# Layer 1 experts of a two-layer metaformer: token tiles loaded in quarters of channels and turned by VectorE in squares of 32

## The chip, the cores and the metric

The kernel runs on one core of a Trainium2 chip. The metric is the device time of one execution in microseconds (us); lower is better. A core has five engines, each working through its own queue of instructions in order: TensorE (PE in the profile) multiplies matrices, VectorE (DVE) and ScalarE (ACT) work elementwise, GpSimd (POOL) does odd work and issues indirect DMAs, and SyncE (SP) issues ordinary DMAs. They wait for each other through semaphores. SBUF is the on-chip memory of 128 partitions, PSUM the banks that TensorE writes.

## The reference, cut to what matters

```python
# layer 1, after a selective scan; x is [4, 256, 32, 32], t its tokens [4 * 1024, 256]
t = t + _L1_ffn_ref(_ln_t(t), Wr, br, ln_g, ln_b, W1, b1, W2, b2)

def _L1_ffn_ref(x, ...):            # 8 experts, 256 channels, 1024 hidden
    logits = xt @ Wr + br
    top_p, top_idx = jax.lax.top_k(softmax(logits), 2)
    weights = top_p / top_p.sum(axis=-1, keepdims=True)
    xn = (xt - mu) * rsqrt(var + 1e-5)
    xe = xn[None] * ln_g[:, None] + ln_b[:, None]
    h = gelu(xe @ W1[e] + b1[e])
    y = h @ W2[e] + b2[e]
    out = weighted sum of y of the two experts of each token
```

The kernel works an expert only on the tokens that chose it.

## The kernel before

Layer 0 and the scan of layer 1 take the first 3362 us and are left alone but for one copy (below). Tokens live channels-first; `norm()` subtracts the mean, turns 128 tokens at a time with TensorE into PSUM (`nm_tp`, L1701), copies them to `tok` with ScalarE (L1705), squares them for the variance (`nm_sq`, L1709) and makes the two factors `nm_s` with powers on GpSimd (`nm_ve`, `nm_s`, L1713 to L1721); ScalarE then scales `tok` (L1725). `route()` picks the two best experts with some fifty small VectorE instructions and an exp on ScalarE (L1605 to L1678), and works out a slot for each token and choice. `scatter()` (L1981) writes rows of 258 numbers (256 channels, and two that say where the result goes) to their slots in DRAM, `slots_x`, with 16 indirect DMAs for each of the 4 batches. Batches 0 to 2 are normalised, routed and scattered during the scan.

A tile is a block of T = 256 slots of one expert. 17 early tiles need only the first three batches. Between them the last batch is normalised, routed and scattered, as a generator (`routing`) that is stepped six times after each early tile. Then come 19 late tiles, and three that run only if a count asks for them.

For each tile, `slots()` loads 256 slots of 258 numbers with one DMA of 258 KB (`xa` for early, `xs` for late tiles; all 17 early loads are issued up front, each with its own buffer). `weights()` loads the expert's w1 and w2 of 1 MB each and its small vectors, two tiles ahead. `inputs()` turns the slots into channels-first with four TensorE transposes (`tp`, L2254) into PSUM, and VectorE applies the expert's gain and shift in two instructions, one for each 128 channels (`xe`, L2257), and works out the result's row numbers `to` (L2260). `hidden()` is 32 matmuls `hp` (L2269) and 8 Gelus `hid` (L2271); `result()` is 32 matmuls `yp` (L2277), one VectorE addition `ys` (L2280), and two indirect DMAs by GpSimd to `results` (L2282), of which the second waits for the first. At the end `results` is loaded again, weighted, turned and added to x.

The order within each queue is set when the program is built: a scheduler places the instructions, starting from the order in which the code calls them.

Of the kernel before, what the change touches and what calls it, by code (L numbers as in the profile page):

```python
# [21 lines left out]
P = 128  # L22
# [15 lines left out]
NS = 16  # L38
SCALE = KD ** -0.5
T = 256  # L40
NTILE = 2 * B * L // T + E - 1
USUAL = 2 * B * L // T + E // 2
BLOCKS = B * L // T
# [19 lines left out]
def metaformer(ctx: ExitStack, tc: tile.TileContext, t: dict, out: bass.AP):  # L63
# [168 lines left out]
    class Routing0:  # L232

        def __init__(self, b, bank, space):
            self.b, self.bank, self.space = b, bank, space
# [236 lines left out]
    with ExitStack() as st:  # L472
# [393 lines left out]
        class Pair:  # L866
# [41 lines left out]
            def norm(self):  # L908
                if self.g == 0 and self.a == 0:
                    self.image.att = wk.tile([P, CT, L], F32, tag="att", name="att")  # L910
                rden = p2.tile([P, L], F32, tag="w", name="rden", bufs=1)[:, : 2 * P]
                nc.vector.reciprocal(rden, self.o_ps[:, 1])
                nc.vector.tensor_tensor(self.image.att[:, self.g, ts(self.a, 2 * P)], self.o_ps[:, 0], rden, ALU.mult)
# [682 lines left out]
    def route(b, tok, slot, space, psum, tag):  # L1596
# [74 lines left out]
        else:  # L1671
# [5 lines left out]
            ends = late.fill(room, tiles, done)  # L1677
            nc.vector.tensor_scalar(extra, ends[0:1, E - 1 : E], USUAL - EARLY + 0.5, None, ALU.is_gt)  # L1678

    def norm(b, tok, pool, psum, tag, raw_tag, d):  # L1680

        rw = rw1
        for h in range(NHALF):
            cols = ts(h, HALF)
            mean = psum.tile([P, HALF], F32, tag=tag, name="nm_mean")
            for c in range(CT):
                nc.tensor.matmul(mean, mean_w, x[b][:, c, cols], start=(c == 0), stop=(c == CT - 1))  # L1689
            yield  # L1690
            for c in range(CT):
                nc.vector.tensor_tensor(d[:, c, cols], x[b][:, c, cols], mean, ALU.subtract)
            yield
        var = pool.tile([P, NT], F32, tag="nm_var", name="nm_var")
        for r in range(NT // 2):
            tp = psum.tile([P, 2, C], F32, tag=tag, name="nm_tp")
            raw = psum.tile([P, HALF], F32, tag=raw_tag, name="raw")[:, : 2 * E].rearrange("p (n e) -> p n e", e=E)
            for i in range(2):
                n = 2 * r + i
                for c in range(CT):  # L1700
                    nc.tensor.transpose(tp[:, i, ts(c, P)], d[:, c, ts(n, P)], ident)  # L1701
                for c in range(CT):
                    nc.tensor.matmul(raw[:, i], d[:, c, ts(n, P)], rw[:, c, :], start=(c == 0), stop=(c == CT - 1))  # L1703
            yield
            nc.scalar.copy(tok[:, ts(r, 2), :C], tp)  # L1705
            for i in range(2):
                n = 2 * r + i
                squares = pool.tile([P, C], F32, tag="nm_sq", name="nm_sq")
                nc.scalar.activation(squares, tp[:, i], AF.Square, scale=C ** -0.5, accum_out=var[:, n : n + 1])  # L1709
            nc.scalar.copy(lg1[:, ts(r, 2)], raw)  # L1710
            yield
        ve, s1, s2 = (pool.tile([P, NT], F32, tag=f"nm_{i}", name=f"nm_{i}") for i in ("ve", "s1", "s2"))
        nc.gpsimd.tensor_scalar(ve, var, 1e-5, None, ALU.add)  # L1713
        nc.gpsimd.tensor_tensor(s1, ve, minus_half, ALU.pow)  # L1714
        yield
        yield
        nc.gpsimd.tensor_tensor(ve, s1, s1, ALU.mult)
        nc.gpsimd.tensor_tensor(ve, ve, var, ALU.mult)
        nc.gpsimd.tensor_scalar(ve, ve, 1e-5, None, ALU.add)
        nc.gpsimd.tensor_tensor(s2, ve, minus_half, ALU.pow)  # L1720
        nc.gpsimd.tensor_tensor(s2, s2, s1, ALU.mult)  # L1721
        nc.vector.tensor_tensor(lg1, lg1, s1.unsqueeze(2).to_broadcast([P, NT, E]), ALU.mult)
        yield
        for n in range(NT):
            nc.scalar.mul(tok[:, n, :C], tok[:, n, :C], s2[:, n : n + 1])  # L1725
        yield
# [247 lines left out]
    nc.vector.memset(count, 0.0)  # L1974
    nc.vector.memset(done, 0.0)

    def scatter(b):

        for n in range(NT):
            for k in range(2):  # L1980
                nc.gpsimd.indirect_dma_start(  # L1981
                    out=slots_x, out_offset=bass.IndirectOffsetOnAxis(ap=slot[:, k, n : n + 1], axis=0),
                    in_=tok[:, n], in_offset=None)
                yield


    with ExitStack() as st:
# [22 lines left out]
        class Scan:  # L2010
# [29 lines left out]
            def inputs(self):  # L2040

                if not self.k:
                    self.uu = lead.uu
                    return
                self.uu = p2.tile([P, 2, L], F32, tag="uu", name="uu")
                nc.gpsimd.tensor_tensor(self.uu[:, 0], self.prep.dx[:, self.c], self.bb, ALU.mult)  # L2046
                nc.scalar.copy(grid(self.uu[:, 1]), cols_flipped(self.uu[:, 0]))
# [166 lines left out]
    with ExitStack() as st:  # L2214
        of_tiles = st.enter_context(ExitStack())
        pb = of_tiles.enter_context(tc.tile_pool(name="m1_b", bufs=2))
        blocks = slots_x.rearrange("(k a p) c -> k p a c", a=T // P, p=P)

        class Tile:
            def __init__(self, tiles, i, tag="xs", bufs=4):  # L2220
                self.tiles, self.i = tiles, i
                self.xs = pb.tile([P, T // P, W], F32, tag=tag, name=tag, bufs=bufs)

            def register(self, k, most):
                return nc.values_load(self.tiles.which[0:1, k, self.i : self.i + 1], engines=[mybir.EngineType.SP],
# [2 lines left out]

            def slots(self):
                block = self.register(1, E * BLOCKS)  # L2230
                nc.sync.dma_start(self.xs, blocks[bass.ds(block, 1)].rearrange("o p a c -> p (o a) c"))

            def weights(self):
                e = self.register(0, E - 1)
# [10 lines left out]
                self.b2 = pb.tile([P, C], F32, tag="b2e", name="b2e")  # L2245
                nc.sync.dma_start(self.b2, t["b2_1"][bass.ds(e, 1)].rearrange("o d -> (o d)").partition_broadcast(P))

            def inputs(self, ps_t):


                tp = ps_t.tile([P, CT, T], F32, tag="tp", name="tp")
                for a in range(T // P):
                    for c in range(CT):
                        nc.tensor.transpose(tp[:, c, ts(a, P)], self.xs[:, a, ts(c, P)], ident)  # L2254
                self.xe = pb.tile([P, CT, T], F32, tag="xe", name="xe")
                for c in range(CT):
                    nc.vector.tensor_scalar(self.xe[:, c], tp[:, c], self.lng[:, c : c + 1],  # L2257
                                            self.lnb[:, c : c + 1], ALU.mult, ALU.add)
                self.to = pb.tile([P, T // P], I32, tag="to", name="to", bufs=NTILE)
                nc.vector.scalar_tensor_tensor(self.to, self.xs[:, :, C + 1], self.tiles.expert[:, self.i : self.i + 1],  # L2260
                                               self.xs[:, :, C], ALU.not_equal, ALU.add)

            def hidden(self, ps_h):
                self.hid = pb.tile([P, NF, T], F32, tag="hid", name="hid")
# [21 lines left out]
        with ExitStack() as sa:  # L2286
            pa = sa.enter_context(tc.tile_pool(name="m1_a", bufs=1))
            psa = sa.enter_context(tc.tile_pool(name="m1_psa", bufs=1, space=PSUM))
            ps_t = sa.enter_context(tc.tile_pool(name="m1_ps_t", bufs=2, space=PSUM))
            ps_h = sa.enter_context(tc.tile_pool(name="m1_ps_h", bufs=3, space=PSUM))  # L2290
            ps_y = sa.enter_context(tc.tile_pool(name="m1_ps_y", bufs=1, space=PSUM))

            def run(one_tile):
                one_tile.inputs(ps_t)
                one_tile.hidden(ps_h)
                one_tile.result(ps_y)

            todo = [Tile(early, i, "xa", EARLY) for i in range(EARLY)]
            for i in range(EARLY):
                todo[i].slots()  # L2300
                if i < 2:
                    todo[i].weights()
            b = B - 1
            routing = chain(norm(b, tok, pa, psa, "t", "raw", pa.tile([P, CT, L], F32, tag="nm_d", name="nm_d")),
                            route(b, tok, slot, pa.tile([P, NUMBERS], F32, tag="numbers", name="numbers"), psa, "t"), scatter(b))
            for i in range(EARLY):
                run(todo[i])
                if i + 2 < EARLY:
                    todo[i + 2].weights()
                for _ in range(6):  # L2310
                    next(routing, None)
            assert next(routing, "end") == "end"

            def run_late(which):
                for i in which:
                    one_tile = Tile(late, i)
                    one_tile.slots()
                    one_tile.weights()
                    run(one_tile)

            run_late(range(USUAL - EARLY))
            more_tiles = nc.values_load(extra[0:1, 0:1], min_val=0, max_val=1,
                                        skip_runtime_bounds_check_because="a comparison gives 0 or 1")
            with tc.If(more_tiles > 0):
                run_late(range(USUAL - EARLY, NTILE - EARLY))
# [97 lines left out]
```

## Time and profile before

| | us |
|---|---|
| median of 3 runs | 3963.53 (3959.7 to 3966.43) |
| the profiled execution, own time | 3952.81 |
| its span | 3951.0 |
| expert stage, first load to last yp | 3362 to 3903 |
| PE busy, of 481 us (3422 to 3903) | 475.0 |
| DVE, ACT, POOL busy, of the same | 58.1, 123.0, 78.8 |
| TensorE transposes tp, x144 | 0.273 each |
| granted TensorE clock, whole span | 0.876 |
| granted TensorE clock, 3422 to 3903 | 1.00 |

A row of the page's list of groups has the line, the engine, the operation, output and input names with shape, and the count; then the group's busy time in us and the mean of one in ns; then the idle time of the engine just ahead of such instructions and what ended most of it. A line of the timeline has the start in us, the length in us, the same names, and in brackets the idle time before it with its releaser. A timeline line with "x32" is 32 instructions in a row; its length reaches to the end of the last one, which overlaps the start of what follows, so spacing is read from starts.

### The profile page before, as it was taken

How to read it: one execution, taken by the hardware profiler on the slowest of the kernel's cores; microseconds unless marked ns; L12 is line 12 of the kernel's file. 1: busy time of each engine (PE TensorE's matmuls, PEld its weight loads, DVE VectorE, ACT ScalarE, POOL GpSimd, SP SyncE). 2: the span in 40 equal slices, each digit the busy share in tenths (PEclk: the TensorE clock that was granted, in tenths of full speed). 3: DMA queues.
4: the chain of work that ended last, by engine and by line, in shares of the span. 5: the costliest groups of instructions: out<-in, count | busy, mean ns of one | idle time of the engine just before them, and what ended most of it. 6: DMA issues, size and time to landing. Idle time of an engine off the chain costs nothing. (4 is left out here: it accounts for less than half of the span.)

```text
span 3951.0 us, 49637 instructions
## 1 busy us (share of the span) xinstructions
PE 3373.9 (85%) x17330; PEld 1889.9 (48%) x17330; DVE 3017.3 (76%) x5164; ACT 2789.5 (71%) x3738; POOL 1936.6 (49%) x1675
## 2 busy tenths in 40 slices
PE   8378888888788888886697889998998989999996
PEld 5134444534353444543475333443443433788885
DVE  3689899989989898999476899999999999211112
ACT  2889999899989999996244677777767766322222
POOL 0145544675648475575343766556555556121111
PEclk9567887788778777788798999999999999999997
DMA  9400084000000000000384434334334334755555
GB/s 283 121 1 1 1 230 128 1 1 31 12 1 1 1 33 1 1 12 17 97 243 133 142 119 139 118 107 127 120 112 127 125 112 128 223 183 185 189 192 188
DMA packets 241814, 393.71 MB, mean 100 GB/s; under 512 B 31888, under 2 KB 182160, under 8 KB 241424
## 3 DMA queue, kind: packets, MB, share of 16 engines
q1 hardware_dynamic: 218016, 340.54, 28.4%
q0 software_dynamic: 19904, 48.48, 3.8%
q8 instruction: 139, 2.28, 0.2%
q10 hardware_dynamic: 3632, 1.40, 0.1%
q14 instruction: 123, 1.01, 0.1%
HBM read 280.41 MB, written 109.94 MB: 99 GB/s over the span
## 5 line engine op out<-in xcount | busy, mean ns | idle before, releaser
L825 POOL TENSOR_SCALAR dr<-s_n,last 128x1024 bf16<-128x1024 f32 x250 | 715.6, 2880 | 729.5 <-DVE state L853 421.5
L735 ACT ACTIVATE junk_a<-s_n,state 128x1024 int8<-128x1024 f32 x448 | 514.7, 1149 | 23.6 <-DVE state L859 7.3
L2081 POOL TENSOR_TENSOR da_c<-prod,come 128x1024 f32<-128x1024 f32 x128 | 257.5, 2012 | 378.8 <-DVE h L2087 322.7
L739 DVE TENSOR_SCALAR_CACHE_REDUCE junk_v<-s_n,state 128x1024 int8<-128x1024 f32 x320 | 408.6, 1277 | 8.8
L2271 ACT ACTIVATE hid<-hp,b 128x256 f32<-128x256 f32 x288 | 134.1, 474 | 361.1 <-PE hp L2269 361.1
L786 DVE SCALAR_TENSOR_TENSOR w<-s_n,win 128x1024 f32<-128x1024 f32 x256 | 352.0, 1375 | 5.3
L789 DVE MAX8 win<-w 128x8 f32<-128x1024 f32 x256 | 314.5, 1228 | 8.8
L2070 DVE TENSOR_TENSOR_SCAN sum<-da,uu 128x1024 f32<-128x1024 f32 x127 | 289.7, 2281 | 26.5 <-PE sum L2052 19.1
L2092 PE MATMUL sum<-h,ident 128*128 128x512 f32 x512 | 261.4, 635 | 55.6 <-DVE h L2087 52.4
L893 ACT ACTIVATE ex<-sT 128x1024 f32<-128x1024 f32 x256 | 246.9, 1016 | 82.9 <-PE sT L885 82.6
L2046 POOL TENSOR_TENSOR uu<-dx,bb 128x1024 f32<-128x1024 f32 x127 | 303.6, 2390 | 1.7 <-DMA bb<-bc_d 1.6
L735 ACT ACTIVATE junk_a<-s_n,guess 128x1024 int8<-128x1024 f32 x256 | 294.2, 1149 | 7.2
L2063 DVE TENSOR_TENSOR_SCAN h<-da,uu 128x1024 f32<-128x1024 f32 x127 | 288.1, 2269 | 1.0 <-POOL uu L2046 1.0
L2087 DVE TENSOR_TENSOR_SCAN h<-da_c,uu 128x1024 f32<-128x1024 f32 x127 | 288.5, 2272 | 0.0
L2058 PE MATMUL sum<-da_c,ident 128*128 128x512 f32 x512 | 257.2, 626 | 27.3 <-POOL da_c L2081 23.8
L903 PE MATMUL o_ps<-ex,vT 128*32 128x256 f32 x2048 | 236.2, 450 | 50.1 <-ACT ex L893 35.7
L2280 DVE TENSOR_TENSOR ys<-yp,b2e 128x512 f32<-128x512 f32 x36 | 24.9, 691 | 325.7 <-PE yp L2277 325.7
L2030 ACT ACTIVATE da_c<-delta,a_log 128x1024 f32<-128x1024 f32 x128 | 268.0, 2094 | 5.2 <-DMA rows_y<-ys 5.1
L2269 PE MATMUL hp<-xe,w 128*128 128x256 f32 x1152 | 259.0, 383 | 9.4 <-DVE xe L2257 5.9
L2282 POOL DMA_INDIRECT results<-ys,to x72 | 69.3, 963 | 397.0 <-DVE ys L2280 183.6
L769 ACT COPY s_n<-sp 128x1024 f32<-128x1024 f32 x256 | 245.5, 1003 | 23.7 <-PE sp L761 16.0
L2277 PE MATMUL yp<-w2e,hid 128*128 128x256 f32 x1152 | 255.6, 380 | 0.0
(675 smaller groups left out, 7513.9 us busy)
## 6 DMA issues: line engine op xcount, KB each, us to landing
cb<-bc_d SPq DMA_DIRECT2D x128, 512.0 KB, 4.1
bb<-bc_d SPq DMA_DIRECT2D x127, 512.0 KB, 5.0
w<-in_w SPq DMA_DIRECT2D x36, 1024.0 KB, 5.4
w2e<-in_w SPq DMA_DIRECT2D x36, 1024.0 KB, 5.5
slots_x<-zeros SPq DMA_DIRECT2D x1, 33669.0 KB
slots_x<-zeros SPq DMA_DIRECT2D x1, 33282.0 KB
w<-in_w SPq DMA_DIRECT2D x72, 256.0 KB, 3.2
xs<-slots_x SPq DMA_DIRECT2D x36, 261.0 KB, 3.4
```

Source lines behind the costliest of these rows:

```text
L735: nc.scalar.activation(junk, self.row(r), AF.Sign, bias=thr, scale=-1.0, accum_out=u)
L739: nc.vector.tensor_scalar(junk, self.row(r), thr, None, ALU.is_lt, ALU.add, accum_out=u)
L786: nc.vector.scalar_tensor_tensor(w, self.row(r), self.win[:, r, 0:1], self.row(r), ALU.is_gt if r < LAST_DVE else ALU.is_ge, ALU.subtract, ...
L789: nc.vector.max(out=self.win[:, r, 1:], in_=w)
L825: ins = eng.tensor_scalar(dr, self.row(r), self.last[:, r : r + 1], None, ALU.is_lt)
L2030: nc.scalar.activation(grid(self.da_c), cols_flipped(self.prep.delta[:, self.c]), AF.Exp, scale=self.decay)
L2046: nc.gpsimd.tensor_tensor(self.uu[:, 0], self.prep.dx[:, self.c], self.bb, ALU.mult)
L2063: nc.vector.tensor_tensor_scan(rows.rearrange("p r w -> p (r w)"), self.da, self.uu[:, 0], 0.0, ALU.mult, ALU.add)
L2070: nc.vector.tensor_tensor_scan(self.sum[:, ::-1], self.da[:, ::-1], self.uu[:, 0][:, ::-1], 0.0, ALU.mult, ALU.add)
L2087: nc.vector.tensor_tensor_scan(self.hs, self.da_c, self.uu[:, 1], 0.0, ALU.mult, ALU.add)
L2092: nc.tensor.matmul(cols_flipped(self.sum[:, ts(h, HALF)]), ident, grid(self.hs)[:, :, ts(h, half)], start=False, stop=False)
L2269: nc.tensor.matmul(hp[:, f % 2], self.w1[:, c, ts(f, P)], self.xe[:, c], start=(c == 0), stop=(c == CT - 1))
```

## The change

`tok` is stored with its channels reordered, in quarters: first 32 channels of the first half of 128, then 32 of the second half, and so on. ScalarE's copy becomes two copies, one for each half. A tile is loaded with four DMAs, one for each quarter, each into 32 partitions: partition = slot within a group of 32, and 8 such groups of 64 numbers along the row (runs of 256 bytes); a fifth small DMA loads the two extra numbers (`meta`). VectorE turns all of it with one transpose instruction of squares of 32 (`xt`), after which partitions are channels, and then applies gain and shift from SBUF (`xe`). The four TensorE transposes and their two PSUM banks go; `yp` gets a second buffer. There are six `xs` buffers in place of 17 and 4; five tiles' loads are issued up front and the load of tile i + 5 after tile i. The scatters are declared independent of each other. The scatters of the last batch come out of the `routing` generator and begin after the last early load is issued (i = 12). A late tile issues its weights first and its slots second.

```diff
@@ norm()
+    def quarters(a):
+        return a.rearrange("p n (q c i) -> p n c q i", c=CT, i=S)
-            nc.scalar.copy(tok[:, ts(r, 2), :C], tp)
+            for c in range(CT):
+                nc.scalar.copy(quarters(tok[:, ts(r, 2), :C])[:, :, c],
+                               tp[:, :, ts(c, P)].rearrange("p n (q i) -> p n q i", i=S))
@@ scatter()
+    def rows_of_their_own(ins, group):
+        tc.declare_no_dep(ins, group=group, reason="rows of their own")
+        tc.add_to_no_dep_group(group, ins)
-                nc.gpsimd.indirect_dma_start(
+                rows_of_their_own(nc.gpsimd.indirect_dma_start(
...
-                    in_=tok[:, n], in_offset=None)
+                    in_=tok[:, n], in_offset=None).ins, "scatter1")
@@ Tile
-        blocks = slots_x.rearrange("(k a p) c -> k p a c", a=T // P, p=P)
+        width = CT * S
+        pieces = [slots_x[:, ts(q, width)].rearrange("(k i t) c -> k t i c", i=T // S, t=S) for q in range(P // S)]
+        marked = slots_x[:, C:].rearrange("(k a p) c -> k p a c", a=T // P, p=P)
-                self.xs = pb.tile([P, T // P, W], F32, tag=tag, name=tag, bufs=bufs)
-                nc.sync.dma_start(self.xs, blocks[bass.ds(block, 1)].rearrange("o p a c -> p (o a) c"))
+                self.xs = pb.tile([P, T // S, width], F32, tag="xs", name="xs", bufs=AHEAD + 1)
+                for q in range(P // S):
+                    nc.sync.dma_start(self.xs[ts(q, S)], pieces[q][bass.ds(block, 1)].rearrange("o t i c -> t (o i) c"))
+                self.meta = pb.tile([P, T // P, W - C], F32, tag="meta", name="meta", bufs=AHEAD + 1)
+                nc.sync.dma_start(self.meta, marked[bass.ds(block, 1)].rearrange("o p a c -> p (o a) c"))
@@ inputs()
-                tp = ps_t.tile([P, CT, T], F32, tag="tp", name="tp")
-                for a in range(T // P):
-                    for c in range(CT):
-                        nc.tensor.transpose(tp[:, c, ts(a, P)], self.xs[:, a, ts(c, P)], ident)
+                xt = pb.tile([P, T // S, CT, S], F32, tag="xt", name="xt")
+                nc.vector.transpose(xt.rearrange("p i c t -> p (i c t)"), self.xs.rearrange("p i c -> p (i c)"))
                 self.xe = pb.tile([P, CT, T], F32, tag="xe", name="xe")
                 for c in range(CT):
-                    nc.vector.tensor_scalar(self.xe[:, c], tp[:, c], self.lng[:, c : c + 1],
-                                            self.lnb[:, c : c + 1], ALU.mult, ALU.add)
+                    nc.vector.tensor_scalar(self.xe[:, c].rearrange("p (i t) -> p i t", t=S), xt[:, :, c],
+                                            self.lng[:, c : c + 1], self.lnb[:, c : c + 1], ALU.mult, ALU.add)
@@ the early and late tiles
-            ps_t = sa.enter_context(tc.tile_pool(name="m1_ps_t", bufs=2, space=PSUM))
-            ps_y = sa.enter_context(tc.tile_pool(name="m1_ps_y", bufs=1, space=PSUM))
+            ps_y = sa.enter_context(tc.tile_pool(name="m1_ps_y", bufs=2, space=PSUM))
-            for i in range(EARLY):
+            for i in range(AHEAD):
                 todo[i].slots()
                 if i < 2:
                     todo[i].weights()
...
+            sending = scatter(b)
             for i in range(EARLY):
                 run(todo[i])
+                if i + AHEAD < EARLY:
+                    todo[i + AHEAD].slots()
+                else:
+                    assert next(routing, "end") == "end"
+                    for _ in range(6):
+                        next(sending, None)
                 if i + 2 < EARLY:
                     todo[i + 2].weights()
                 for _ in range(6):
                     next(routing, None)
...
             def run_late(which):
                 for i in which:
                     one_tile = Tile(late, i)
+                    one_tile.weights()
                     one_tile.slots()
-                    one_tile.weights()
                     run(one_tile)
```

More of the change, by code (lines that the diff above doesn't have):

```diff
@@ L40 @@
 T = 256
+S = 32
+AHEAD = 5
 NTILE = 2 * B * L // T + E - 1
@@ L2216, in metaformer, with __init__ @@
         pb = of_tiles.enter_context(tc.tile_pool(name="m1_b", bufs=2))
-        blocks = slots_x.rearrange("(k a p) c -> k p a c", a=T // P, p=P)
+        width = CT * S
+        pieces = [slots_x[:, ts(q, width)].rearrange("(k i t) c -> k t i c", i=T // S, t=S) for q in range(P // S)]
+        marked = slots_x[:, C:].rearrange("(k a p) c -> k p a c", a=T // P, p=P)
         class Tile:
-            def __init__(self, tiles, i, tag="xs", bufs=4):
+            def __init__(self, tiles, i):
                 self.tiles, self.i = tiles, i
-                self.xs = pb.tile([P, T // P, W], F32, tag=tag, name=tag, bufs=bufs)
             def register(self, k, most):
@@ L2246, in weights, with inputs @@
                 nc.sync.dma_start(self.b2, t["b2_1"][bass.ds(e, 1)].rearrange("o d -> (o d)").partition_broadcast(P))
-            def inputs(self, ps_t):
-                tp = ps_t.tile([P, CT, T], F32, tag="tp", name="tp")
-                for a in range(T // P):
-                    for c in range(CT):
-                        nc.tensor.transpose(tp[:, c, ts(a, P)], self.xs[:, a, ts(c, P)], ident)
+            def inputs(self):
+                xt = pb.tile([P, T // S, CT, S], F32, tag="xt", name="xt")
+                nc.vector.transpose(xt.rearrange("p i c t -> p (i c t)"), self.xs.rearrange("p i c -> p (i c)"))
                 self.xe = pb.tile([P, CT, T], F32, tag="xe", name="xe")
                 for c in range(CT):
-                    nc.vector.tensor_scalar(self.xe[:, c], tp[:, c], self.lng[:, c : c + 1],
-                                            self.lnb[:, c : c + 1], ALU.mult, ALU.add)
+                    nc.vector.tensor_scalar(self.xe[:, c].rearrange("p (i t) -> p i t", t=S), xt[:, :, c],
+                                            self.lng[:, c : c + 1], self.lnb[:, c : c + 1], ALU.mult, ALU.add)
                 self.to = pb.tile([P, T // P], I32, tag="to", name="to", bufs=NTILE)
-                nc.vector.scalar_tensor_tensor(self.to, self.xs[:, :, C + 1], self.tiles.expert[:, self.i : self.i + 1],
-                                               self.xs[:, :, C], ALU.not_equal, ALU.add)
+                nc.vector.scalar_tensor_tensor(self.to, self.meta[:, :, 1], self.tiles.expert[:, self.i : self.i + 1],
+                                               self.meta[:, :, 0], ALU.not_equal, ALU.add)
             def hidden(self, ps_h):
@@ L2288, in metaformer @@
             psa = sa.enter_context(tc.tile_pool(name="m1_psa", bufs=1, space=PSUM))
-            ps_t = sa.enter_context(tc.tile_pool(name="m1_ps_t", bufs=2, space=PSUM))
             ps_h = sa.enter_context(tc.tile_pool(name="m1_ps_h", bufs=3, space=PSUM))
-            ps_y = sa.enter_context(tc.tile_pool(name="m1_ps_y", bufs=1, space=PSUM))
+            ps_y = sa.enter_context(tc.tile_pool(name="m1_ps_y", bufs=2, space=PSUM))
             def run(one_tile):
-                one_tile.inputs(ps_t)
+                one_tile.inputs()
                 one_tile.hidden(ps_h)
                 one_tile.result(ps_y)
-            todo = [Tile(early, i, "xa", EARLY) for i in range(EARLY)]
-            for i in range(EARLY):
+            todo = [Tile(early, i) for i in range(EARLY)]
+            for i in range(AHEAD):
                 todo[i].slots()
@@ L2304, in metaformer @@
             routing = chain(norm(b, tok, pa, psa, "t", "raw", pa.tile([P, CT, L], F32, tag="nm_d", name="nm_d")),
-                            route(b, tok, slot, pa.tile([P, NUMBERS], F32, tag="numbers", name="numbers"), psa, "t"), scatter(b))
+                            route(b, tok, slot, pa.tile([P, NUMBERS], F32, tag="numbers", name="numbers"), psa, "t"))
+            sending = scatter(b)
             for i in range(EARLY):
                 run(todo[i])
+                if i + AHEAD < EARLY:
[4 more added lines that the diff above has]
+                        next(sending, None)
                 if i + 2 < EARLY:
@@ L2311, in metaformer @@
                     next(routing, None)
-            assert next(routing, "end") == "end"
+            assert next(sending, "end") == "end"
             def run_late(which):
```

## The prediction, made before the changed kernel ran

> **What bounds the kernel now.** I read the page first: its slices, its chain and its costliest groups. In the last slices TensorE (PE) is at 9 tenths while VectorE (DVE) and ScalarE (ACT) are at 1 to 3. The groups say the same:
>
> ```profile
> L2269 PE MATMUL hp<-xe,w 128*128 128x256 f32 x1152 | 259.0, 383 | 9.4 <-DVE xe L2257 5.9
> ...
> L2277 PE MATMUL yp<-w2e,hid 128*128 128x256 f32 x1152 | 255.6, 380 | 0.0
> ```
>
> 1152 is 36 tiles of 32, so 36 tiles run. Before hp PE is idle for 9.4 us in all, before yp never. The expert stage (3362 to 3903 us) is TensorE's, at a granted clock of 1.00 from 3422 us on. What TensorE does there that is no expert matmul, the timeline of a pair of tiles shows (start, length, engine, line):
>
> ```profile
> 3575.02 7.07 PE L2277 MATMUL yp<-w2e,hid 128*128 128x256 f32 x32
> 3581.92 1.04 PE L2254 MATMUL tp<-ident,xa 128*128 128x128 f32 x8
> 3583.32 7.19 PE L2269 MATMUL hp<-xe,w 128*128 128x256 f32 x32 [0.36 <-DVE xe L2257]
> 3590.35 7.07 PE L2277 MATMUL yp<-w2e,hid 128*128 128x256 f32 x32
> 3597.26 7.09 PE L2269 MATMUL hp<-xe,w 128*128 128x256 f32 x32
> ```
>
> 32 matmuls pass in 6.91 us (3590.35 to 3597.26), so a tile needs 13.83. Between 3581.92 and 3583.32 there are eight transposes, which serve two tiles at once, and 0.36 us of waiting for xe. The second tile of the pair follows with no gap. VectorE at that boundary:
>
> ```profile
> 3582.12 0.69 DVE L2280 TENSOR_TENSOR ys<-yp,b2e 128x512 f32<-128x512 f32 x1 [13.14 <-PE yp L2277]
> 3582.73 1.89 DVE L2257 TENSOR_SCALAR xe<-tp,lng,lnb 128x256 f32<-128x256 f32 x4
> ```
>
> ys starts 0.20 us after TensorE's end, xe stands behind it and starts 0.61 us later. From hp of tile 3 (3422.28) to the end of yp of tile 35 (3902.9) lie 480.6 us: 33 tiles of 13.83 are 456.4, the rest, **24.2 us**, is what transposes and xe waits cost (16 boundaries of 1.5). The one other loss is tile 2, where the last batch is routed:
>
> ```profile
> 3409.95 1.51 PE L2269 MATMUL hp<-xe,w 128*128 128x256 f32 x4 [3.46 <-ACT hid L2271]
> ...
> 3422.28 7.07 PE L2269 MATMUL hp<-xe,w 128*128 128x256 f32 x32
> ```
>
> ```profile
> 3402.74 0.96 POOL L2282 DMA_INDIRECT results<-ys,to  x1 [9.71 <-DVE ys L2280]
> 3404.01 0.24 POOL L1713 TENSOR_SCALAR nm_ve<-nm_var 128x8 f32<-128x8 f32 x1 [0.30 <-ACT nm_sq L1709]
> ...
> 3408.77 0.22 POOL L1721 TENSOR_TENSOR nm_s<-nm_s,nm_s 128x8 f32<-128x8 f32 x1
> 3409.16 1.09 POOL L2282 DMA_INDIRECT results<-ys,to  x1 [0.17 <-DVE numbers L1608]
> ```
>
> hp of tile 2 starts at 3402.01, of tile 3 at 3422.28: 20.3 us for a tile of 13.8, with a little other work, a loss of 6.9. GpSimd (POOL) does the norm's powers between the two result writes of tile 1.
>
> **What the Trainium skill says.** "VectorE: DVE Perf Modes", section The three transpose paths: VectorE turns only blocks of 32x32; 311 ns for 128x128 in bf16. No run here shows VectorE's yet. "Vector Engine (DVE) Microarchitecture Reference", section 3.8, says that the transpose sustains an element per cycle and lane. "TensorE: Matmul & The Clock Gate", Part 4, gives about 275 ns for a TensorE transpose inside a kernel; this trace has 273. Its section Why this matters for your kernels warns of TensorE idle for over some 3 us; the trace agrees: after 3.46 us of idling four hp took 1.51 us, where four otherwise take 0.86.
>
> **The change, part by part.** What decides is the order in which the built program of the changed kernel stands in each engine's queue. I read it from that program.
>
> 1. *Transposes gone from TensorE.* At most the 24.2 us above: **-24.2**.
>
> 2. *What stands ahead of xe on VectorE.* xe must now be ready when yp of the tile before ends. But ys of that tile waits for that same end, and in many tiles stands ahead of xe. Of the 33 boundaries into tiles 3 to 35:
>  - 7 have xe ahead of ys (3, 4, 14 to 18): no wait.
>  - 15 have ys, then both halves of xe (5 to 11, 13, 19, 20, 22, 23, 25, 26, 28). hp waits 0.20 to ys, 0.61 for ys, 0.41 for the first half (128x256 from SBUF to SBUF takes 0.406, the xn row at L1453), 0.06 to be seen, and 0.1 for the second: 1.4 each, 21.0.
>  - 4 have one half ahead (12, 21, 24, 27): 1.05 each, 4.2.
>  - 7 have even the new xt behind ys (29 to 35): 1.4 plus xt, to and the write of xt, on which xe waits. For xt I take 0.7: the nearest row, ys, moves 128x512 in 0.69. From below 0.6 (512 elements at that page's rate, an estimate); from above 1.3 (four times the 311 ns, an estimate). to issues in 0.15, 0.1 for the write: 2.35 each, 16.5 (15 to 21).
>
>  Together **+41.7** (33 to 48). Ahead of ys or not, an xt that isn't behind ys is hidden under 13.8 us of matmuls.
>
> 3. *Tile 2 and the routing.* Two moves. On GpSimd the second result write of tile 1 now stands ahead of nm_ve; it waits for the landing of the first (a to b is 4.7 to 5.3 us in this trace). ys of tile 1 issues about 3402.8; first write 0.95 later, its landing 5.3, second write 1.1, some 0.4 for nm_ve's waits: nm_ve at 3410.5, not 3404.01. On VectorE the whole routing chain now stands ahead of xe of tile 2, which before stood in its middle. The powers take 4.98 to nm_s; eight tok scalings on ScalarE at 0.42 come next, then a table load of 1.28 and exp, 9.9 after nm_ve; the last 29 small VectorE instructions take 4.5 as before (0.7 up to L1638 and 3.8 from L1651 on), to and half of xe 0.6. So hp of tile 2 starts at about 3410.5 + 15.1 = 3425.6, and hp of tile 3 at 3439.4, where it was 3422.28: +17.1. Of this the start (step 4) is 1.0, so **+16.1**. The cold clock after 22 us of idling: **+1** (0.65 in the row above, 0 to 2). Below: +9 if the write lands at once; above: +20.
>
> 4. *Start.* Five loads stand where one did: lnb, on which the first xe waited (1.2 us), is issued about 2.2 us later. ScalarE's table load in tile 0 hides part: **+1.0** at the end of tile 1 (0 to 3).
>
> 5. *tok in two copies.* In the scan ScalarE's tok copy (0.48 to the next) lies on a chain on which VectorE waits; a half copy adds about 0.05, in 12 places: **+0.65** (0 to 2.5).
>
> 6. *Costed at nothing.* Scatters declared independent: in the scan they wait for their place on GpSimd, not for each other. Scatters of the last batch after tile 9: the write they replace is not waited for before tile 17. Late loads with 256 B rows instead of 1032 B: issued when yp two tiles back ends, after w2, b2; w2 lands 5.6 after, I estimate the quarters at 8 to 9.5, and xe two microseconds later, where 13.8 is allowed. "DMA: Bandwidth & Descriptors", Specifications, names 512 B as the least size for line rate; no run here shows its price. Weights ahead of slots on SyncE's (SP's) queue: included. The cover is the tile of matmuls; if it is gone, see the second rival. yp in two buffers frees the bank earlier, but no yp waits now (0.0).
>
> Sum: -24.2 + 41.7 + 16.1 + 1 + 1.0 + 0.65 = **+36.2**. The profiled execution took 3952.81 (its span 3951.0), so 3989.0 in its terms; the median of the runs is 10.7 above it, so **3999.7** there, which I give.
>
> **Rivals.** *The transposes pay in full.* xe is worked out while TensorE multiplies and the routing costs what it did: -24.2 + 1.0 + 0.65 = -22.6, so 3941. For it: VectorE is busy for 58 of 481 us, so it has time. Against: it works in order, and ys can't start before yp ends. It decides if boundaries and the extra loss at tile 2 together come under 13 us, where I count 59. *Late loads come late.* If the quarters land 2 us past need at each of 19 late tiles, 38 more: 4038. For it: 1280 pieces for a tile in place of 256, with the DMA engines half busy (0.56 in this stretch). Against: 3 us of room. *It does half of what I read.* Half of the boundary waits and a routing loss of 5: 3963.5 - 24.2 + 21 + 5 + 2.6 = 3968, no change.
>
> **How the numbers follow.** The order case 0.78, with own range 3982 to 4018 (steps 2 and 3 at their ends, not both at once). Late loads 0.07. No change 0.05. Faster 0.10. The range 3966 to 4026 leaves out about 2 in 10. A measurement of this kernel tells about 0.2%, 7.9 us, from no change. Faster 0.10, within 0.2% 0.05, slower 0.85.
>
> **What would show it.** Right: no tp; hp's idle near 60 us, ended by xe; a gap of some 22 us ahead of hp of tile 2; nm_ve behind two result writes; gaps of 1.4 at tiles 5 to 13 and over 2 at tiles 29 to 35, with ys just ahead of xe or xt. Wrong: hp idle below 15 us; nm_ve within 2 us of ys of tile 1; xt waiting for xs in the late tiles; or xt over 1.3 us.

## The result, and the profile after

The changed kernel is slower: 3994.16 us at the median of 4 runs, where the kernel before has 3964.45 beside it; the ratio is 1.0075 (95% interval 1.0053 to 1.0097). 36 us were forecast and 30 came. The profiled execution took 3985.1 (span 3983.4), 32.3 more than that of before.

The costliest groups of the page after, in the lines that answer to those of before. The expert matmuls are as many and nearly as long (the mean of hp goes from 383 to 387 ns, by a slower clock in two tiles); what has grown is the idle time ahead of hp, from 9.4 to 37.5 us, and xe ends nearly all of it:

```profile
L2282 PE MATMUL hp<-xe,w 128*128 128x256 f32 x1152 | 264.1, 387 | 37.5 <-DVE xe L2270 37.4
...
L2290 PE MATMUL yp<-w2e,hid 128*128 128x256 f32 x1152 | 255.3, 379 | 0.0
```

The stage starts with the first nm_mean (3361.63 before, 3361.73 after) and ends with the last yp (3902.7 and 3934.8, each the start of its last piece and the usual spacing of 0.22), so nearly all of the difference is made in it. Below, "excess" of a tile is the time from its first hp to the next tile's first hp, less the 13.83 us of its matmuls, read off the timeline. Tiles are counted from 0.

TensorE's timeline of the changed kernel around tile 2. Only small groups of matmuls (nm_tp and sums among them) stand in a gap that reaches from 3402 to 3425; then hp of tile 2 takes 9.05 us where 7.07 is usual:

```profile
3395.23 7.07 PE L2290 MATMUL yp<-w2e,hid 128*128 128x256 f32 x32
3402.13 0.60 PE L1706 MATMUL nm_tp<-ident,nm_d 128*128 128x128 f32 x4
...
3416.30 0.66 PE L1631 MATMUL sums<-numbers,before 128*128 128x64 f32 x2 [11.29 <-DVE numbers L1625]
...
3425.23 9.05 PE L2282 MATMUL hp<-xe,w 128*128 128x256 f32 x32 [7.84 <-DVE xe L2270]
3434.12 7.07 PE L2290 MATMUL yp<-w2e,hid 128*128 128x256 f32 x32
3441.03 7.07 PE L2282 MATMUL hp<-xe,w 128*128 128x256 f32 x32
```

GpSimd at the same place: both result writes of tile 1 now come ahead of nm_ve, which starts at 3410.53 and not at 3404.01:

```profile
3403.30 0.96 POOL L2295 DMA_INDIRECT results<-ys,to  x1 [9.50 <-DVE ys L2293]
3409.54 0.96 POOL L2295 DMA_INDIRECT results<-ys,to  x1 [5.28 <-DMA meta<-slots_x]
3410.53 0.25 POOL L1720 TENSOR_SCALAR nm_ve<-nm_var 128x8 f32<-128x8 f32 x1
```

VectorE at the end of the routing chain: its last instruction, then to, then xe, on which TensorE has been waiting:

```profile
3424.56 0.17 DVE L1593 CAST late_which<-numbers 1x22 int32<-1x22 f32 x1
3424.65 0.20 DVE L2273 SCALAR_TENSOR_TENSOR to<-meta,early_expert 128x2 int32<-128x2 f32 x1
3424.78 0.72 DVE L2270 TENSOR_SCALAR xe<-xt,lng,lnb 128x256 f32<-128x256 f32 x2
```

Then a boundary of the late tiles on VectorE (the start of tile 29), with ys, xt, to and xe in a row, and the same boundary on TensorE. yp of tile 28 ends at 3821.67 (3814.60 and 7.07), ys starts 0.04 us later, and in VectorE's queue all that tile 29 needs stands behind it:

```profile
3821.71 0.69 DVE L2293 TENSOR_TENSOR ys<-yp,b2e 128x512 f32<-128x512 f32 x1 [13.74 <-PE yp L2290]
3822.32 0.70 DVE L2267 STREAM_TRANSPOSE xt<-xs 128x512 f32<-128x512 f32 x1
3822.94 0.18 DVE L2273 SCALAR_TENSOR_TENSOR to<-meta,late_expert 128x2 int32<-128x2 f32 x1
3823.06 0.74 DVE L2270 TENSOR_SCALAR xe<-xt,lng,lnb 128x256 f32<-128x256 f32 x2
```

```profile
3814.60 7.07 PE L2290 MATMUL yp<-w2e,hid 128*128 128x256 f32 x32
3823.52 7.19 PE L2282 MATMUL hp<-xe,w 128*128 128x256 f32 x32 [1.85 <-DVE xe L2270]
```

The idle time in brackets counts from the end of the last piece of yp, the excess from starts; so 1.85 us of idling is an excess of 2.12 here.

### The profile page after: what moved, and what is told of

Same layout as the page of the kernel before. It is cut to its first block, busy times and chain, and to the rows that moved or that the text cites. A ratio compares the mean times of both kernels' runs of the same rounds, so it can differ in the third digit from the quotient of the medians.

```text
span 3983.4 us, 49863 instructions
## 1 busy us (share of the span) xinstructions
PE 3364.6 (84%) x17186; PEld 1874.1 (47%) x17186; DVE 3030.2 (76%) x5200; ACT 2791.8 (70%) x3754; POOL 1933.0 (49%) x1675
## 3 DMA queue, kind: packets, MB, share of 16 engines
q14 instruction: 128, 1.05, 0.1%
## 5 line engine op out<-in xcount | busy, mean ns | idle before, releaser
L2282 PE MATMUL hp<-xe,w 128*128 128x256 f32 x1152 | 264.1, 387 | 37.5 <-DVE xe L2270 37.4
```

The source lines that it names most:

```text
L2282: nc.tensor.matmul(hp[:, f % 2], self.w1[:, c, ts(f, P)], self.xe[:, c], start=(c == 0), stop=(c == CT - 1))
```

## The experiments

The start of the stage moves between executions by up to 23 us (3358.65 to 3381.83 in the profiles below), with code ahead of it that does the same work. So a single profile is read within the stage, and whole times are compared over several runs. The table has the profiles, in us; "stage" is from the first nm_mean to the end of the last yp.

| kernel | excess, tiles 0 to 2 | excess, tiles 3 to 35 | of it a hold-up of hid | stage | whole, ratio to before |
|---|---|---|---|---|---|
| before | 9.8 | 24.1 | | 541.1 | |
| changed | 28.3 | 37.4 | | 573.1 | 1.0075 (1.0053 to 1.0097) |
| e_ahead | 28.4 | 16.9 | 16.8 | 552.8 | 1.0029 (1.0016 to 1.0042) |
| e_route | 6.9 | 49.4 | about 13 | 563.7 | 1.0055 (1.0036 to 1.0074) |
| e_best | 7.6 | 18.6 | 17.5 | 534.3 | 0.9975 (0.9965 to 0.9985) |
| e_best_spaced | 6.5 | 1.1 | | 516.8 | 0.9937 (0.9919 to 0.9954) |
| e_best_serial | 6.7 | 22.2 | | 537.9 | 0.9984 (0.9972 to 0.9997) |
| e_spaced | 28.3 | 35.8 | | 573.0 | 1.0067 (1.0050 to 1.0084) |
| e_pool | 24.6 | 37.4 | | 569.4 | one run |
| e_dve | 22.3 | 37.6 | | 567.4 | one run |
| e_xt_twice | 28.2 | 52.9 | about 15 | 590.2 | one run |
| e_inputs_only | 26.9 | 9.7 | | 554.0 | 1.0021 (1.0010 to 1.0031) |
| e_before_route | 10.0 | 25.2 | | 543.3 | 0.9999 (0.9987 to 1.0010) |

**The boundaries alone (e_ahead).** `inputs()` of the next tile is called ahead of `result()`, and ys is held behind xe within VectorE's queue (NoSync stands for the kind of dependency: an order within one queue, with no semaphore):

```diff
-                one_tile.inputs()
+                if not one_tile.turned:
+                    one_tile.inputs()
                 one_tile.hidden(ps_h)
-                one_tile.result(ps_y)
+                if following is not None and not following.turned:
+                    following.inputs()
+                one_tile.result(ps_y, following)
...
+                tc.add_manual_dep(add.ins, following.xe_done.ins.name, NoSync)
```

> The changed kernel, in which on VectorE ys of each tile from tile 2 on is held behind xe of the tile after it (an order within the engine, no new wait on another engine). My theory (the queue's order makes the boundary waits): the 15 waits of 1.39 us and 7 of 2.13 us go, 35.8 us in all, perhaps also the slow hp of tile 32 (1.7); the gap ahead of hp of tile 2 stays near 22 us. So about 3957 us where the changed kernel has 3994, and 0.2% below the kernel before. Rival one (late loads): the room is used up by the quarters, xt waits for xs in the late tiles and ys with it; time over 3975. Rival two (VectorE's order is not what TensorE waits on): the waits stay, 3994.

The boundary waits are gone: 32 of the 33 tiles from 3 on have an excess of 0.02 us or less. But the whole is 3979, not 3957, since tile 13 has an excess of 16.8 that the changed kernel doesn't have. For ScalarE's waits in this stretch the profile names no releaser ("remote" is an end near which it has no instruction's end; the numbers are the total in us, how often, and the longest; more on it under e_best):

```profile
ACT hid L2284 <- remote: 16.8, 4, 5.9
```

So the order theory is shown for the boundaries, and neither rival foresaw what came in their place.

**Tile 2 alone (e_route).** Three orders are set within queues: nm_ve to nm_s ahead of the second result write of tile 1, the scaling of the logits, from which the routing's chain on VectorE hangs, behind xe of tile 3, and the tok scalings behind hid of tile 2. The part of the edit in the loop over early tiles:

```diff
+                if i == 1:
+                    if not hasattr(todo[2], "xe"):
+                        todo[2].inputs()
+                    todo[3].inputs()
+                    held["xe"] = todo[3].xe_done
+                    todo[2].hidden(ps_h)
+                    held["hid"] = todo[2].gelu
+                    while "powers" not in held:
+                        next(routing)
+                    todo[1].send()
```

> The changed kernel with three orders set around tile 2: nm_ve to nm_s on GpSimd ahead of the second result write of tile 1; the routing's VectorE chain behind xe of tiles 2 and 3; the tok scalings on ScalarE behind hid of tile 2. Boundaries are left as they are. My theory: hp of tile 2 starts at 3404 to 3406 and not at 3425, runs at the full clock, hp of tile 3 starts near 3419 in place of 3441; 22 us less, 3972. Rival (another wait takes its place: ScalarE's exp, or the chain ahead of xe of tile 4): hp of tile 3 or 4 waits for what the routing still holds, and less than 10 us is gained, over 3984.

The excess of tiles 0 to 2 falls from 28.3 to 6.9, 21.4 less, where 22 was expected. The whole is 3986 and not 3972: the same hold-up, at tiles 12 and 13, takes some 13 us back.

**Both (e_best), and the kernel before with the order of tile 2 (e_before_route).**

> Both orders together, and xe of the next tile ahead of ys from tile 0 on. My theory: the two effects add, 36 to 38 at the boundaries and 23 to 25 at tile 2: 60 us under the changed kernel, about 3934, and 0.992 of the kernel before; what is left over before is then the 24.2 us of transposes and xe waits, and the 6.9 of tile 2. Rival (late loads, or a shared limit such as TensorE's clock): less than 45 us in all.

> The kernel before, with the same three orders around tile 2 and nothing else. My theory: of its 6.9 us of loss there 5 to 6 go, so 3958 where it has 3964; the 24.2 us of transposes stay. Set beside e_best it gives the worth of the turn on VectorE when the order is right: some 24 us. Rival (the turn on VectorE is worth little, the order all): e_best within 10 us of this one.

e_best is faster than both kernels, by 38 us against the changed one where 60 was expected; 17.5 of the missing 22 are in tile 13 (which the expectation of e_best_spaced, below, calls tile 12). ScalarE's timeline of e_best there: hid comes every 5 us, where 0.86 is usual:

```profile
3570.48 0.47 ACT L2292 ACTIVATE hid<-hp,b 128x256 f32<-128x256 f32 x1 [7.62 <-PE hp L2290]
3575.42 0.48 ACT L2292 ACTIVATE hid<-hp,b 128x256 f32<-128x256 f32 x1 [4.46 <-remote]
3581.06 0.47 ACT L2292 ACTIVATE hid<-hp,b 128x256 f32<-128x256 f32 x1 [5.17 <-remote]
3586.72 0.47 ACT L2292 ACTIVATE hid<-hp,b 128x256 f32<-128x256 f32 x1 [5.18 <-remote]
```

TensorE in the same tile:

```profile
3569.09 3.05 PE L2290 MATMUL hp<-xe,w 128*128 128x256 f32 x12
3575.95 2.78 PE L2290 MATMUL hp<-xe,w 128*128 128x256 f32 x8 [3.81 <-issue]
3581.59 2.07 PE L2290 MATMUL hp<-xe,w 128*128 128x256 f32 x4 [2.86 <-ACT hid L2292]
3589.39 3.78 PE L2290 MATMUL hp<-xe,w 128*128 128x256 f32 x8 [5.73 <-ACT hid L2292]
```

The two wait for each other. The trace tells more than "remote": each of the last three hid waits for the semaphore that TensorE's pieces raise, and that semaphore's next step is recorded 0.03 us before hid starts (3575.39, 3581.04, 3586.70). Yet the last pieces that TensorE had started before those times started at 3571.76, 3578.10 and 3583.03, 2.9 to 3.7 us earlier. So ScalarE isn't held by work of its own; the word that hp is done comes late. Whether the pieces ended late or only the signal did, the trace can't tell, since ends of matmuls are modelled. TensorE's three stops make up 12.4 of the 17.5 us; most of the rest is its granted clock, 0.50 from 3577 to 3594.

Meanwhile GpSimd issues the 16 scatters of the last batch, 3563 to 3583, one each 1.27 us.

e_before_route gained nothing, against the 5 to 6 us expected: the excess of tile 2 fell from 6.4 to 4.1, but tile 0 has 5.4 in place of 3.0 and tile 3 2.6 in place of 1.4. e_best lies 10 us under it and not 24, at the edge of what the rival allowed; without the hold-up (e_best_spaced, next) it is 25, by the ratios 0.9937 and 0.9999.

**The burst (e_best_spaced, e_spaced).** The scatters are spread: four behind the result writes of each of tiles 11 to 14, so that they take 47 to 48 us rather than 20 to 22.

```diff
                 rows_of_their_own(ins, "scatter1")
+                if earlier[0] is not None:
+                    tc.add_manual_dep(ins, earlier[0].ins.name, NoSync)
...
-                    for _ in range(6):
+                    earlier[0] = todo[i - 1].sent
+                    for _ in range(4):
                         next(sending, None)
```

> e_best with the 16 scatters of the last batch spread: four behind the result writes of each of tiles 11 to 14, where e_best issues them in a burst of some 21 us. In the profile of e_best four hid of tile 12 start 3 to 6 us late with no releaser that the profile shows, while the burst runs; that tile takes 31.3 us in place of 13.8. Theory (the burst holds ScalarE up): no such tile any more, 17 us less than e_best's 3956, so about 3940, and 0.993 of the kernel before. Rival one (the hold-up has another cause, such as loads or instruction fetch): it stays, or comes at another tile, 3956. Rival two (scatters later, so late loads late): xt of tile 17 waits for xs by over 3 us.

> The changed kernel with its scatters spread in the same way and nothing else. The changed kernel's own profile shows no hold-up of hid, but its runs lie between 3985 and 4000. If the burst holds ScalarE up in part of its executions, this one is faster by up to 10 us, with runs nearer to each other; if the hold-up needs the order of e_best, it is 3994 as before.

3941.5 where 3940 was expected, and the fastest of all these kernels. The page's hp row has nearly no idle time left:

```profile
L2297 PE MATMUL hp<-xe,w 128*128 128x256 f32 x1152 | 257.9, 381 | 0.7 <-ACT hid L2299 0.7
```

With no scatter in a burst the hold-up is gone, so the burst brings it about in this order of the queues; that it does so by way of ScalarE, as the expectation says, isn't shown. In the changed kernel itself spreading changes nothing (3994.4, 3983.7 to 3996.9), so its own 30 us owe nothing to the burst. Of seven profiles with the burst four show the hold-up (e_ahead, e_route, e_best, e_xt_twice) and three do not (changed, e_pool, e_dve); of the three with spread or serial scatters none does.

**Scatters one after the other (e_best_serial).** The declaration that they are independent is left out for the last batch:

```diff
-                rows_of_their_own(ins, "scatter1")
+                if b < B - 1:
+                    rows_of_their_own(ins, "scatter1")
```

> e_best with the scatters of the last batch dependent on each other again (each waits for the landing of the one before, as in the kernel before); they still begin only after the last early load. Theory: no hold-up of hid at tiles 12 and 13, but 16 landings of some 4 to 5 us end about 80 us after tile 11, so the loads of tile 17 start late and hp of tile 17 waits 15 to 30 us: 3950 to 3965, no better than e_best. Rival (landings overlap with loads anyway): no wait at tile 17, 3940 as with the scatters spread.

As expected: no hold-up, but the waits of VectorE and of TensorE in the stage show the late tile that pays, tile 17, with an excess of 18.8 at its start. 3955.2, no better than e_best.

```profile
DVE xt L2277 <- DMA xs<-slots_x: 155.4, 19, 30.5
```

```profile
PE hp L2292 <- DVE xe L2280: 18.6, 1, 18.6
```

In each line the numbers are the total in us, how often, and the longest. So with this order, and scatters that start only in tile 12, the declaration is needed, and it is what lets them come as a burst.

**The links at tile 2, one by one (e_pool, e_dve).** e_pool sets GpSimd's order only, e_dve VectorE's only.

> The changed kernel with only GpSimd's order set: nm_ve to nm_s ahead of the second result write of tile 1. Read within the stage, against the changed kernel, where tile 1's hp to tile 2's hp takes 23.2 us more than 13.83. My theory: nm_ve starts 6.2 to 6.5 us earlier, all that hangs on it moves with it, and the gap falls by the same 6 to 6.5, to about 17. Rival (the second write is not on the path): the gap stays at 23.

nm_ve starts 44.9 us after the stage's start and not 48.8, and the excess of tile 1 falls from 23.2 to 19.2. Both moved by 4, not by 6 to 6.5, for nm_ve now meets the next thing that it needs, the last nm_sq:

```profile
3403.59 0.24 POOL L1726 TENSOR_SCALAR nm_ve<-nm_var 128x8 f32<-128x8 f32 x1 [2.40 <-ACT nm_sq L1722]
```

> The changed kernel with only VectorE's order set: xe of tiles 2 and 3 ahead of the routing. My theory: hp of tile 2 starts at once (excess of tile 1 some 3 us), but ScalarE still holds hid of tile 2 behind the tok scalings, which wait for nm_s; TensorE stops after six pieces until some 8.4 us after nm_ve plus 5, and the excess of tiles 1 and 2 together falls from 25 to 13 to 17. Rival (VectorE's order alone is the loss at tile 2): it falls to 5 or less.

hp of tile 2 starts at once and then stops where it was expected to, after six pieces:

```profile
3424.95 1.46 PE L2290 MATMUL hp<-xe,w 128*128 128x256 f32 x6
3439.53 8.06 PE L2290 MATMUL hp<-xe,w 128*128 128x256 f32 x22 [13.12 <-ACT hid L2292]
```

The excess of tiles 1 and 2 falls from 25.2 to 19.2, where 13 to 17 was expected: after 13 us of idling 22 pieces took 8.06, in e_best_spaced 5.02. GpSimd's order alone gains 4 us, VectorE's alone 6, all three together 21. ScalarE's share is read from the wait of 13.12 us above; no run sets its order alone, or leaves it alone out.

**The turn twice (e_xt_twice).**

```diff
-                nc.vector.transpose(xt.rearrange("p i c t -> p (i c t)"), self.xs.rearrange("p i c -> p (i c)"))
+                for _ in range(2):
+                    nc.vector.transpose(xt.rearrange("p i c t -> p (i c t)"), self.xs.rearrange("p i c -> p (i c)"))
```

> The changed kernel with every turn on VectorE done twice, the second writing the same values again: 36 more of 0.71 us. In its built order one turn stands ahead of ys and one behind at tiles 29 to 35, so as many turns as before lie behind ys. Theory (only what stands behind ys costs): the boundaries grow by less than 3 us in all. Rival (VectorE's work counts wherever it stands): 25 us more.

One run, 4008.0, but 15.7 of it is an excess at tile 13 with the hold-up of hid. Without it tiles 3 to 35 have 37 us, the changed kernel 37.4. So in this one profile 36 more turns cost nothing that can be seen where VectorE has the time; the turn by itself is not the loss.

**The loads and the turn alone (e_inputs_only).** The quarters, `meta`, xt, xe and the two tok copies are put into the kernel before; the loop, the 17 loads up front, the scatters within the routing and yp's one buffer stay as they were.

> The kernel before with only the quarters, the turn on VectorE and the two tok copies: all 17 early loads up front, scatters one after the other within the routing, yp in one buffer, late slots ahead of late weights, all as before. In its built order the routing stands ahead of ys of tile 0 on VectorE, xe stands ahead of ys up to tile 27, and ys ahead of xe at tiles 28, 29 and 31 to 35 (7 waits of 1.4, one of less). 85 loads of about 0.55 us each stand ahead of w1 of tile 2 on SyncE, so hp of tile 2 starts 10 to 17 us later than in the kernel before. Theory (order, not the turn, makes the cost): the 24.2 us of transposes go, 10 come back at the boundaries, the start costs 5 to 17 and the 6.9 of tile 2 go: 3948 to 3962. Rival (the turn on VectorE is itself the loss): 3985 or more, with waits at all boundaries.

The boundaries are as expected: 9.7 in place of 24.1, with seven waits of about 1.3 to 1.4. The start is worse than expected: the first hp comes 19.5 us after the stage's start in place of 9.3, tile 0 has an excess of 11.0 and tile 1 of 13.9, for which hp waits 13.6 for xe, and 3976 is outside the 3948 to 3962 given. The order theory holds for the boundaries; that the turn is itself the loss has no support here. How the 27 us of the start divide between SyncE's 85 loads and the routing ahead of ys of tile 0 was not separated.

## Why the prediction was right

It read the order of the queues and priced what stood ahead of what. Point by point:

1. *Transposes gone, -24.2.* Right as an upper bound: in e_best_spaced tiles 3 to 35 have an excess of 1.1 where before has 24.1. The changed kernel doesn't collect it.
2. *Boundaries, +41.7.* Measured 37.4. The 15 with ys ahead of both halves of xe cost 1.27 to 1.38 as read off the timeline; 1.4 was given. The 7 with xt behind ys cost 2.1, not 2.35: xt takes 0.71, but the next instruction starts 0.62 after it. The 4 with one half ahead cost 0.1 and not 1.05: this term was wrong, since in those tiles the built program also has the hp pieces of the first half put ahead of those of the second, which covers ys and the second xe (the first hid starts 2.05 us after the first hp there, in tiles without a wait 1.11). TensorE's order within the tile wasn't read. And one late tile (32) cost 1.7 more, by the clock (last section).
3. *Tile 2, +16.1, and +1 for the clock.* nm_ve at 3410.5, measured 3410.53; hp of tile 2 at 3425.6, measured 3425.23. That nm_ve agrees to 0.03 is luck: the first write started 0.45 us earlier than forecast (3403.30, since step 4 cost less), the second 6.24 after it and not 5.3, and 0.5 less went to the second write and the wait behind it. The chain itself is as described. The clock cost 1.9 and not 1: hp of tile 2 takes 8.89 from start to start, usually 6.9 to 7.0, with a granted clock of 0.50 from its start to 3429.07. So hp of tile 3 starts at 3441.03 and not at 3439.4. The 0.65 that the forecast rested on sets a length with its last piece in full against a spacing; from start to start the four pieces took 1.30 (3409.95 to 3411.25), 0.44 more than 0.86. That GpSimd and VectorE both hold tile 2 is shown by e_pool and e_dve, that the three orders together free it by e_route.
4. *Start, +1.0.* The end of tile 1 moved by 0.56.
5. *tok in two copies, +0.65.* The stage starts 0.1 later, but with starts that spread over 23 us this says nothing; it stays open.
6. *Costed at nothing.* Late loads: right for TensorE. xe of tile 17 is done at 3641.1 and hp needs it at 3645.7, 4.6 us later; at tile 18 it is 4.4 us. But xt does wait for xs in 12 of the 19 late tiles, up to 7.1 us, which the prediction had named as a sign of being wrong. Nothing that TensorE needs is late by it, so the sign was badly chosen (total in us, how often, longest):

```profile
DVE xt L2267 <- DMA xs<-slots_x: 80.2, 12, 7.1
```

   Scatters: right in the changed kernel, where they start at 3582.75, in tile 12. In e_ahead, e_route, e_best and e_xt_twice their burst cost 12 to 17 us. Since e_xt_twice keeps all of the changed kernel's waits, it isn't shown that these waits are what keeps the hold-up away.

Sum: +36.2 was forecast and the stage has +32.0; the four half-ahead boundaries (-3.8) are most of the difference. The other misses at boundaries cancel in part, which is luck: the seven with xt were set 1.6 too high, and the clock of tile 32, in no term of the sum, added 1.7. That hp's idle time would be near 60 us was not met in the row (37.5), since the gap at tile 2 is put down in part to sums and nm_tp, which stand in it, and the row has 1.10 and 1.85 of idling for an excess of 1.37 and 2.12. Of the rivals, the full pay-off is what the kernel would do with another order: e_best_spaced has 3941.5 where that rival has 3941. Late loads did not come late, but in e_best_serial, where the scatters ahead of them did.

## What to carry to other kernels

Work moved from the busiest engine to an idle one pays only if the idle engine can do it before the moment it is needed: in an in-order queue, an instruction that waits for the end of this tile (ys) must not stand ahead of one that the next tile starts with (xe). Read the built order of every queue that the moved work touches, with long chains of small instructions (the routing) above all, and price each wait from its head. When a wait is taken away, look at what it had kept apart: here the waits between the scatters had kept 16 indirect DMAs from coming as a burst.

## What the runs showed of the hardware

- VectorE's turn of 128x512 numbers of 4 bytes in squares of 32 took 0.700 to 0.714 us (36 of them). An instruction that doesn't read its result could start 0.62 to 0.63 after it; xe, which does, 0.75 after it.
- A burst of 16 independent indirect DMAs by GpSimd in some 20 us can make TensorE's word to ScalarE come late: hid waited 3 to 8 us for it, two to four times in a row. Spread over 47 us it didn't. It was seen in four of seven profiles with a burst; by what mechanism, and why not in the others, is open.
- TensorE's granted clock fell in some tiles after waits of only 1.85 us, where the Trainium skill ("TensorE: Matmul & The Clock Gate", Why this matters for your kernels) warns of idle gaps above some 3 us; here shorter ones were followed by a fall in a few cases. Tile 32 of the changed kernel, in stretches of 2 us (the columns are the stretch, its length, the busy time of PE, PEld, DVE, ACT and POOL, the granted clock, the DMA share and GB/s):

```profile
3872.00:3874.00 2.00, 2.00 (x8) 1.63 (x7) 0.00 (x0) 0.64 (x2) 0.00 (x0) 0.70 1.07 378
3874.00:3876.00 2.00, 2.00 (x6) 1.60 (x5) 0.00 (x0) 0.77 (x2) 0.00 (x0) 0.50 1.10 295
3876.00:3878.00 2.00, 2.00 (x10) 1.70 (x10) 0.00 (x0) 0.80 (x3) 0.96 (x1) 0.95 0.16 33
```

  hp of that tile took 8.86 us; the other six with the same wait took 7.19. It happened in e_pool (tile 34) and e_dve (tile 35) too, and not in e_route, e_spaced or e_xt_twice: after 3 of 40 such waits in six profiles, so it can't be counted on either way. The traffic of the DMAs isn't what decides: in the first four us of hp it was as high at five of the other six tiles (327 to 346 GB/s, at tile 32 331), and at tile 35 of e_dve the clock fell at 66 GB/s. In e_best_spaced, where hp waits 0.7 us in all, the clock was 1.00 from 3411 us to the end of the stage.
